# Rearranging the last part of a fused state-space and feed-forward kernel: an early quarter of a convolution, dense weights in four buffers, four dense products beside the last output product

## The chip, the cores and the metric

The kernel runs on one core of a Trainium2 chip as one launch. The metric is the device time in microseconds (us). Before the change it is 1575.42 us, the median of three runs (1573.84 to 1576.71).

## What is computed

The reference has two residual layers. The first mixes tokens with a gated state-space block, the second is a dense layer behind a grouped convolution, with a mask:

```python
# x: (64 sequences, 32 positions, 512 channels), float32
def reference(x, cond, ...):
    # layer 1: per-sequence 32x32 mixing, in-projection to 10304 channels, causal
    # convolution of 4 taps, SiLU, scan over 32 positions, gate, norm, out-projection
    x = x + attn(cond_mix(x, cond))
    # layer 2
    c2 = conv1d(x, weight9, groups=4) + cond @ c_weight.T + bias   # along the channels
    dots = softmax(c2 @ centroids.T / 0.1)                         # 64 centroids
    hits = dots > 0.01
    query_sel = any(hits, over centroids)        # one flag per token
    cluster_sel = any(hits, over all tokens)     # one flag per centroid
    row_sel = cluster_sel[assignments]           # one flag per output channel
    dense = c2 @ weight.T + ffn_bias
    return x + where(query_sel & row_sel, dense, 0)
```

`row_sel` needs the hits of all 2048 tokens, so no output can be written before the last token has been routed.

## The kernel before

**Layer 1.** The tokens are worked in 4 groups of 512 (T = 0 to 3), the 4096 inner channels in 8 groups (g = 0 to 7). That is 32 steps, i = 8 T + g. A step runs ten chunks (`chunk(i, c)`): each is a product of 12 matmuls (three passes over four 128-row pieces, because every float32 operand is split into a high and a low part), followed by an activation and, for eight of ten kinds, by tap or gate work on DVE and ACT. Between the chunks the step places the work of the step before it: `yend` (DVE multiplies the scan's result y by the gate, ACT makes the high part `yhi`, DVE subtracts to get `ylo`), `sumsq`, and the out-projection `out_step(i, 0..3)`, whose result `outp_end` adds to the accumulator `acc`. `inner(c)` places smaller things after chunk c: `gram`, the scan (L492), `decay`. `y_part` makes y in two halves.

**Order.** For PE and SP (the queue that issues nearly all DMAs) the order of the instructions is the order in which the program is written. On DVE, ACT and POOL a scheduler decides it when the program is built. Every engine and the SP queue execute in order: an instruction that waits holds all behind it on its engine.

**Buffers.** SBUF tiles with one tag share a fixed number of buffers; a new tile waits until the tile that held the buffer has been read for the last time. For what follows these matter: `raw` (4 buffers), `wsp` (7, the weights of the chunks), `y2` (3), `y` (3), `B` and `C` (2 each), `x` (4), `z` (6). PSUM has seven banks under the tag `mm` and one under `gs`.

**Layer 2, the tail.** It begins after step 31. 16 tiles of 128 tokens are numbered j = 0 to 15; a quarter is four tiles.
- `outp_end` of the steps with g = 7 stores `acc` to DRAM twice: as it is (`x1_d`, by POOL's queue) and turned (`x1p_d`, L669; in the last group 16 stores by SP).
- `p_load(j)` (L686) loads a turned tile, `conv(js)` (L758) runs the convolution of two or four tiles on PE and DVE adds the context (`c2s`, L768). `c2_xpose(j)` (L784) turns the tile back on PE; ACT makes the high part (L792) and DVE the low part (L793).
- `route(T)` multiplies a quarter with the centroids, `route2(T)` makes softmax, hits and `qsel` (the flag of each token).
- `asg_i` (L1011) loads the assignments; DVE makes from them `asg_f`, `oh` and `oh2`, a one-hot table (both in tag `B`).
- `dense(j)` is the dense product of tile j, 12 matmuls of about 2.7 us in all. `dense_kept` copies the result from PSUM to SBUF.
- After the last quarter's `route2`, 16 small matmuls count the hits (`cnt_ps`), another spreads the selected clusters (`r_ps`, L1076), ACT copies this to `rsel` and DVE makes `bm` = bias x rsel.
- `finish(j)`: DVE runs three instructions of 128x512: x1 += bm x qsel (L1085), d = dense x qsel x rsel (L1089), d += x1 (L1090); SP stores d.

In the kernel before, all 16 tiles' convolution lies behind the last chunk of step 31. The list `units` holds the order of the convolution, transposes and routing, and two dense products (tiles 0 and 1) are kept. The other 14 come after the last convolution:

```python
    j = NI - 1
    unit(1); y_part(j, 8, 16); unit(1)          # conv(0, 1), second half of y, conv(2, 3)
    ...yend, sumsq...
    unit(5); unit(2)                            # conv(4..7), four transposes, conv(8..11), route(0)
    for bg in range(4): out_step(j, bg)
    for k in range(4): unit(2); ...load and split dense weights wf[:, k]...
```
(line breaks are changed here.)

Of the kernel before, what the change touches and what calls it, by code (L numbers as in the profile page):

```python
# [7 lines left out]
F32 = mybir.dt.float32  # L8
# [24 lines left out]
def mamba_block_kernel(  # L33
# [641 lines left out]
    attend(0)  # L675
    w_ahead(-1)

    p_of, c2_of, ffn = {}, {}, {"next": 0}
    hits = {}

    def p_load(j):
        pr = sb.tile([P, 4, 130], F32, tag="wsp", name=f"pr{j}", bufs=7)
        T, jj = divmod(j, 4)
        nc.vector.memset(pr[:, :, 0:1], 0.0)
        nc.vector.memset(pr[:, :, 129:130], 0.0)
        nc.sync.dma_start(out=pr[:, :, 1:129], in_=x1p_d[T][jj])  # L686
        p_of[j] = pr
# [31 lines left out]
        for r in range(4):  # L719
            nc.vector.tensor_copy(cr[:, r], o[:, r])  # L720

    def split_load(src, shape, name, tg, bufs):
        raw = sb.tile(shape, F32, tag="raw", name=name + "r", bufs=4)
        nc.sync.dma_start(out=raw, in_=src)
        hi = sb.tile(shape, F32R, tag=tg, name=name + "h", bufs=bufs)
        lo = sb.tile(shape, F32R, tag=tg, name=name + "l", bufs=bufs)
        nc.scalar.copy(hi, raw)
        nc.gpsimd.tensor_tensor(lo, raw, hi.bitcast(F32), ALU.subtract)
        ffn[name] = (hi, lo)

    def ffn_start():
        ffn["qsel"] = const.tile([P, 16], F32, tag="qsel", name="qsel")

    def c2_tiles(T):
        if T < 2:
# [3 lines left out]
        return tuple(  # L739
            sb.tile([P, 4, TOK], F32R, tag=tg, name=f"c2_{T}_{tg}", bufs=nb) for tg, nb in tags  # L740
        )

    def p_more(n):
        for _ in range(n):
            j = ffn["next"]
            if j < 12:
                p_load(j)
                ffn["next"] = j + 1

    def conv(js):  # L750
        src = [p_of.pop(j) for j in js]
        o = [bank(f"cv{j}") for j in js]
        for d in range(3):
            for j, s, t in zip(js, src, o):
                for q in range(4):
                    at = 32 * ((q + j) % 4)
                    rows = slice(32 * q, 32 * q + 32)
                    nc.tensor.matmul(  # L758
                        t[at : at + 32].rearrange("p (b m) -> p b m", b=4),
                        lhsT=tww[rows, d, :],  # L760
                        rhs=s[rows, :, d : d + 128],
                        start=d == 0,
                        stop=d == 2,
                    )
        for j, t in zip(js, o):
            tg, nb = (("B", 2), ("C", 2), ("x", 4))[2 if j // 4 % 2 else j % 2]
            c2 = sb.tile([P, 4, P], F32, tag=tg, name=f"c2s{j}", bufs=nb)
            nc.vector.tensor_tensor(  # L768
                c2,
                t.rearrange("p (b m) -> p b m", b=4),  # L770
                ctxr[:, j].unsqueeze(2).to_broadcast([P, 4, P]),
                ALU.add,
            )
            ffn[("c2", j)] = c2
        p_more(len(js))

    def c2_xpose(j):
        T, jj = divmod(j, 4)
# [32 lines left out]
    def route2(T):  # L811
# [20 lines left out]
        nc.vector.tensor_scalar(hit, d, THRESHOLD, None, ALU.is_gt)  # L832
        nc.vector.tensor_reduce(ffn["qsel"][:, 4 * T : 4 * T + 4], hit, AX.X, ALU.max)
        hits[T] = hit

    def at(f, *a):
        return lambda: f(*a)

    units = [at(conv, (0, 1)), at(conv, (2, 3)), at(conv, (4, 5, 6, 7))]
    units += [at(c2_xpose, j) for j in range(4)]  # L840
    units += [at(conv, (8, 9, 10, 11)), at(route, 0)]
    units += [at(c2_xpose, j) for j in range(4, 8)]
    units += [at(route2, 0), at(route, 1)]
    units += [at(c2_xpose, j) for j in range(8, 12)]
    units += [at(route2, 1), at(route, 2)]
    units += [lambda j=j: dense_kept(j) for j in range(2)]
    units += [at(conv, (12, 13, 14, 15)), at(route2, 2)]
    units += [at(c2_xpose, j) for j in range(12, 16)]

    def unit(n=1):  # L850
        for _ in range(n):
            units.pop(0)()

    NI = NT * NG

# [27 lines left out]
    for i in range(NI):  # L883
# [9 lines left out]
        def inner(c):  # L893
            nonlocal wo_steps
            if c in (1, 2, 3, 4):
                if c < 4:
                    wo_split()
                next(wo_steps, None)
            if c in (5, 6):
                wo_store()  # L900
            if c == 6 and i + 1 < NI and (i + 1) % NG:
                da_load(i + 1)
            if c == 8:
                wo_steps = wo_pieces(i)
                for _ in range(1 if i + 1 < NI else 4):
                    next(wo_steps)
            if c == 3 + late:
                gram(i)
            if c == 4:
                flip(i, 0)  # L910
                if i:
                    scan(i)
            if c == 7:
                gram_rows(i)
                decay(i)
            if i == NI - 1 and c > 4:
                p_more(1)

        chunk(i, 0)
        if i and g == 0:  # L920
# [54 lines left out]
        step_more()  # L975
        if i == NI - 3:
            turned_setup()
            ffn_start()
        chunk(i, 9)
        inner(9)  # L980
        flip(i, 3)
# [1 line left out]
        step_more()  # L983
        y_part(i, 0, 8)

    j = NI - 1
    unit(1)
    y_part(j, 8, 16)
    unit(1)
    for c in range(4):  # L990
        yend(j, c)
    sumsq(j)
    split_load(cent, [P, 4, 64], "ct", "z", 6)
    unit(5)
    unit(2)
    for bg in range(4):
        out_step(j, bg)

    wf_t = sb.tile([P, 2, 4, DM], F32R, tag="wo", name="wf_t", bufs=1)
    wf_hi, wf_lo = wf_t[:, 0], wf_t[:, 1]  # L1000
    for k in range(4):
        unit(2)
        wr = sb.tile([P, DM], F32, tag="raw", name=f"wfr{k}", bufs=4)
        nc.sync.dma_start(out=wr, in_=wf[:, k, :])
        nc.scalar.copy(wf_hi[:, k, :], wr)
        nc.gpsimd.tensor_tensor(wf_lo[:, k, :], wr, wf_hi[:, k, :].bitcast(F32), ALU.subtract)

    for j in range(12, 16):
        p_load(j)
    asg_i = sb.tile([64, DM], mybir.dt.int32, tag="y2", name="asg_i", bufs=3)  # L1010
    nc.sync.dma_start(out=asg_i, in_=asg.partition_broadcast(64))  # L1011
    cl = const.tile([64, 2], F32, tag="cl", name="cl")
    nc.sync.dma_start(out=cl, in_=cl_in)
    asg_f = sb.tile([64, DM], F32, tag="y2", name="asg_f", bufs=3)
    nc.vector.tensor_copy(asg_f, asg_i)
    br = sb.tile([P, 2, DM], F32, tag="da", name="br", bufs=1)
    bias_b, rsel = br[:, 0], br[:, 1]
    nc.sync.dma_start(out=bias_b, in_=bf.partition_broadcast(P))
    oh = sb.tile([64, DM], BF16, tag="B", name="oh", bufs=2)
    nc.vector.tensor_scalar(oh, asg_f, cl[:, 0:1], None, ALU.is_equal)  # L1020
    oh2 = sb.tile([64, DM], BF16, tag="B", name="oh2", bufs=2)
    nc.vector.tensor_scalar(oh2, asg_f, cl[:, 1:2], None, ALU.is_equal)
    nc.vector.tensor_tensor(oh, oh, oh2, ALU.max)

    fo, x1t = {}, {}

    def x1_load(j):
        T, jj = divmod(j, 4)
# [7 lines left out]
    def dense(j, lo=0, hi=DM):  # L1036
        T, jj = divmod(j, 4)
        cols = slice(128 * jj, 128 * jj + 128)
        c2_hi, c2_lo = c2_of[T]
        o = bank(f"fo{j}_{lo}")[:, : hi - lo]  # L1040
        mm_split(
            o,
            lambda k: c2_hi[:, k, cols],
            lambda k: c2_lo[:, k, cols],
            lambda k: wf_hi[:, k, lo:hi],
            lambda k: wf_lo[:, k, lo:hi],
            4,
        )
        fo[(j, lo)] = o

    def dense_kept(j):
        dense(j)
        kept = sb.tile([P, DM], F32, tag="z", name=f"kept{j}", bufs=6)
        nc.scalar.copy(kept, fo[(j, 0)])
        fo[(j, 0)] = kept

    unit(len(units))
    for j in range(6):
        x1_load(j)
    route(3)  # L1060
    dense(2)
    route2(3)
    dense(3)
    late_ones, crep = ffn["late"][:, 1024:1152], ffn["late"][:64, 1152:1280]
    cnt_ps = ps.tile([64, 2], F32, tag="gs", name="cnt_ps", bufs=1)
    for n in range(16):
# [4 lines left out]
    csel = const.tile([64, 1], F32, tag="csel", name="csel")  # L1071
    nc.vector.tensor_scalar(csel, cnt_ps[:, 0:1], 0.5, None, ALU.is_gt)
    nc.vector.tensor_scalar(crep, late_ones[:64, :], csel, None, ALU.mult)
    dense(4)
    r_ps = ps.tile([P, DM], F32, tag="gs", name="r_ps", bufs=1)
    nc.tensor.matmul(r_ps, lhsT=crep, rhs=oh, start=True, stop=True)  # L1076
    nc.scalar.copy(rsel, r_ps)
    bm = sb.tile([P, DM], F32, tag="dt", name="bm", bufs=1)
    nc.vector.tensor_tensor(bm, bias_b, rsel, ALU.mult)

    def finish(j, lo=0, hi=DM):
        q = ffn["qsel"][:, j : j + 1]
        o = fo.pop((j, lo))
        x1 = x1t[j]
        nc.vector.scalar_tensor_tensor(  # L1085
            x1[:, lo:hi], bm[:, lo:hi], q, x1[:, lo:hi], ALU.mult, ALU.add
        )
        d = sb.tile([P, hi - lo], F32, tag="y", name=f"fd{j}_{lo}", bufs=3)
        nc.vector.scalar_tensor_tensor(d, o, q, rsel[:, lo:hi], ALU.mult, ALU.mult)  # L1089
        nc.vector.tensor_tensor(d, d, x1[:, lo:hi], ALU.add)  # L1090
        nc.sync.dma_start(
            out=out[4 * j : 4 * j + 4].rearrange("b s d -> (b s) d")[:, lo:hi], in_=d
        )

    for j in range(4, 16):
        if j + 2 < 16:
            x1_load(j + 2)
        finish(j - 4)
        if 4 < j < 15:
            dense(j)  # L1100
    dense(15, 0, 256)
    for j in range(12, 15):
        finish(j)
    dense(15, 256, 512)
    finish(15, 0, 256)
    finish(15, 256, 512)
# [96 lines left out]
```

## Time and profile before

| what | value |
|---|---|
| median of three runs | 1575.42 us |
| time of the profiled execution | 1577.95 us |
| its span, first to last instruction | 1576.2 us |
| granted TensorE clock, mean | 0.987 |
| PE busy, share of the span | 96% |
| DVE / ACT / POOL busy | 75% / 40% / 30% |
| last matmul of step 31's chunks ends | 1462.9 us |
| last matmul of the kernel ends | 1571.1 us |
| last DVE instruction ends | 1573.4 us |

A profile line of the timeline gives the start, the busy time, the engine, the source line, what is written and read, the number of instructions and, in brackets, the idle time ahead of them and what ended it. In a table by windows, each engine has its busy time in the window and the number of instructions. A row of the chain of waits has a start, a length and the engine whose work, or wait, the chain passes through. "issue" is waiting for which the profile shows no other cause.

### The profile page before, as it was taken

How to read it: one execution, taken by the hardware profiler on the slowest of the kernel's cores; microseconds unless marked ns; L12 is line 12 of the kernel's file. 1: busy time of each engine (PE TensorE's matmuls, PEld its weight loads, DVE VectorE, ACT ScalarE, POOL GpSimd, SP SyncE). 2: the span in 40 equal slices, each digit the busy share in tenths (PEclk: the TensorE clock that was granted, in tenths of full speed). 3: DMA queues.
4: the chain of work that ended last, by engine and by line, in shares of the span. 5: the costliest groups of instructions: out<-in, count | busy, mean ns of one | idle time of the engine just before them, and what ended most of it. 6: DMA issues, size and time to landing. Idle time of an engine off the chain costs nothing.

```text
span 1576.2 us, 35828 instructions
## 1 busy us (share of the span) xinstructions
PE 1519.7 (96%) x14963; PEld 1246.4 (79%) x14963; DVE 1180.3 (75%) x1877; ACT 629.4 (40%) x1122; POOL 476.7 (30%) x446
## 2 busy tenths in 40 slices
PE   6789999999999999999999999999999999999898
PEld 5567888788778888888888888888888888888567
DVE  5677777788866777977877777877877777777658
ACT  4455564455433333434433333434433333333230
POOL 6266665554341112222141112223141112222110
PEclk9789999999999999999999999999999999999999
DMA  5566888677575555555575555655575555554454
GB/s 190 175 237 212 308 309 292 194 233 279 185 241 184 176 171 179 198 191 171 191 241 190 165 180 169 209 176 175 187 245 188 170 181 167 182 179 139 119 164 167
DMA packets 124033, 311.71 MB, mean 198 GB/s; under 512 B 30880, under 2 KB 42400, under 8 KB 121824
## 3 DMA queue, kind: packets, MB, share of 16 engines
q1 hardware_dynamic: 121056, 302.08, 57.0%
q0 software_dynamic: 2816, 7.34, 1.4%
q8 instruction: 118, 1.93, 0.5%
q14 instruction: 43, 0.35, 0.1%
HBM read 237.54 MB, written 71.83 MB: 196 GB/s over the span
## 4 chain that ended last, share of the span: by engine, by line
PE 69%; DVE 17%; issue 4%; ACT 4%; POOL 3%; DMA 2%; SPq 1%; POOLq 0%; ACTq 0%; DVEq 0%
PE mm L192 42%; PE o L192 17%; PE y L549 5%; DVE x L447 3%; DVE ylo L577 2%; DVE src L492 1%; PE g_ps L503 1%; DVE acc L659 1%; DMA w<-in_win_dram 1%; DVE C L447 1%; DVE src L533 1%; POOL wsp L401 1%; DVE xs L463 1%; PE fo L192 1%; PE gr_ps L515 1%
## 5 line engine op out<-in xcount | busy, mean ns | idle before, releaser
L192 PE MATMUL mm<-hid,wsp 128*128 128x512 f32 x3840 | 931.6, 396 | 0.0
L192 PEld LDWEIGHTS mm<-hid,wsp 128*128 128x128 f32 x3840 | 721.1, 190 | 151.3 <-issue 1.0
L573 POOL TENSOR_TENSOR y<-y,y 128x512 f32<-128x512 f32 x96 | 145.3, 1514 | 547.9 <-ACT y L563 543.2
L447 DVE SCALAR_TENSOR_TENSOR x<-mm,xw,x 128x496 f32<-128x496 f32 (+2 forms) x384 | 272.2, 709 | 26.0 <-ACT x L443 20.9
L192 PE MATMUL o<-wo,yhi 128*128 128x512 f32 x1024 | 279.2, 394 | 8.8 <-POOL wo L631 6.2
L455 ACT ACTIVATE x<-x 128x512 f32<-128x512 f32 x128 | 81.0, 632 | 378.4 <-DVE x L447 355.1
L192 PEld LDWEIGHTS o<-wo,yhi 128*128 128x128 f32 x1024 | 190.2, 188 | 49.1 <-POOL wo L631 7.9
L447 DVE SCALAR_TENSOR_TENSOR B<-mm,pack,B 128x496 f32<-128x496 f32 (+2 forms) x96 | 68.7, 716 | 175.5 <-ACT B L443 173.3
L577 DVE TENSOR_TENSOR ylo<-z,yhi 128x512 fp32r<-128x512 f32 x128 | 141.4, 1108 | 1.0 <-ACT yhi L576 1.0
L443 ACT ACTIVATE x<-mm,xb,xw 128x512 f32<-128x512 f32 x128 | 99.7, 779 | 94.5 <-PE mm L192 93.5
L192 PE MATMUL o<-wo,ylo 128*128 128x512 f32 x512 | 137.1, 390 | 0.0
L549 PEld LDWEIGHTS y<-src,xs 32*64 32x64 f32 x8192 | 91.1, 132 | 41.9 <-issue 25.6
L463 DVE STREAM_TRANSPOSE xs<-x 128x512 f32<-128x512 f32 x128 | 89.8, 701 | 45.9 <-ACT x L455 43.5
L659 DVE SCALAR_TENSOR_TENSOR acc<-o,r,acc 128x512 f32<-128x512 f32 x128 | 95.3, 745 | 34.8 <-POOL r L601 30.3
L549 PE MATMUL y<-src,xs 32*64 32x32 f32 x8192 | 99.6, 227 | 18.1 <-DVE src L533 6.7
L601 POOL TENSOR_TENSOR r<-var,mhalf 128x4 f32<-128x4 f32 x32 | 33.2, 1039 | 269.4 <-DVE var L597 269.4
L192 PEld LDWEIGHTS o<-wo,ylo 128*128 128x128 f32 x512 | 96.1, 188 | 20.4 <-DVE ylo L577 0.2
L565 DVE SCALAR_TENSOR_TENSOR z<-y,pack,z 128x512 f32<-128x512 f32 x128 | 94.5, 742 | 19.3 <-ACT y L563 19.3
L401 POOL TENSOR_TENSOR wsp<-w,wsp 128x512 fp32r<-128x512 f32 x56 | 77.7, 1400 | 98.8 <-ACT wsp L400 69.7
L576 ACT CAST yhi<-z 128x512 fp32r<-128x512 f32 x128 | 78.9, 619 | 52.3 <-DVE z L565 52.2
L436 ACT ACTIVATE z<-mm 128x512 f32<-128x512 f32 x128 | 75.9, 593 | 56.4 <-PE mm L192 56.4
L447 DVE SCALAR_TENSOR_TENSOR C<-mm,pack,C 128x496 f32<-128x496 f32 (+2 forms) x96 | 68.8, 716 | 16.5 <-ACT C L443 14.3
(195 smaller groups left out, 1350.5 us busy)
## 6 DMA issues: line engine op xcount, KB each, us to landing
wsp<-wsp SPq DMA_DIRECT2D x320, 512.0 KB
wo<-wos SPq DMA_DIRECT2D x96, 512.0 KB
da<-da SPq DMA_DIRECT2D x128, 128.0 KB
wos<-wo SPq DMA_DIRECT2D x16, 1024.0 KB
w<-in_win_dram SPq DMA_DIRECT2D x48, 256.0 KB
wor<-in_wout_dram SPq DMA_DIRECT2D x32, 256.0 KB
xr<-in_win_dram SPq DMA_DIRECT2D x24, 256.0 KB
acc<-in_x_in_dram SPq DMA_DIRECT2D x4, 1024.0 KB
```

What stands on the lines that cost most here:

```text
L192: nc.tensor.matmul(o, lhsT=a(k), rhs=b(k), start=j == 0, stop=j == last)
L401: nc.gpsimd.tensor_tensor(lo, w, hi.bitcast(F32), ALU.subtract)
L443: nc.scalar.activation(t, o, AF.Identity, bias=bias, scale=taps[:, 3:4])
L447: nc.vector.scalar_tensor_tensor(tv[:, :, d:], ov[:, :, : L - d], taps[:, 3 - d : 4 - d], tv[:, :, d:], ALU.mult, ALU.add,)
L455: nc.scalar.activation(t, t, AF.Silu)
L463: nc.vector.transpose(st["xs"][:, :, k], t.rearrange("p (n t) -> p n t", t=L))
L549: nc.tensor.matmul(st["y"][q][64 * f : 64 * f + 64, 32 * n : 32 * n + 32], lhsT=st["xs"][r, n, 2 * f : 2 * f + 2].rearrange("p e x -> p (e ...
L565: nc.vector.scalar_tensor_tensor(z, y, nw_s[:, cc : cc + 1], z, ALU.mult, ALU.mult)
L573: st["add"] = nc.gpsimd.tensor_tensor(y2, st["y2"], y2, ALU.add).ins
L576: nc.scalar.copy(hi, z)
L577: st["lo"] = nc.vector.tensor_tensor(lo, z, hi.bitcast(F32), ALU.subtract).ins
L659: nc.vector.scalar_tensor_tensor(acc[:, bg, :], o, st["r"][:, bg : bg + 1], acc[:, bg, :], ALU.mult, ALU.add)
```

## The change

It rearranges the last two steps and the tail:

1. The convolution of tiles 0 to 3 and its transposes move into steps 30 and 31, between chunks. The centroids are loaded and split in step 30.
2. The dense weights have no buffer of their own in `wo` now. They are loaded in two DMAs of two pieces into one buffer `wr` and split into four `wsp` buffers (`wf_of[0..3]`): the first pair in step 31 after chunk 5, the second after chunk 8.
3. `p_load` uses the four `raw` buffers for all tiles but 8, 9 and 10.
4. `route(0)` moves between the two halves of the last y. Behind the second half come four dense products (tiles 0 to 3), then the out-projection, then `conv(4..7)`, the loads of tiles 12 to 15, the loads of assignments and the one-hot table, `conv(8..11)`, and the rest in the order shown.
5. Kept dense results (tiles 0 to 5) get the bias added on the way from PSUM, by DVE instead of ACT's copy. For the tiles from 6 on, `prep` adds bm x qsel to x1, with ACT and POOL. `finish` has two DVE instructions for each tile instead of three.

```diff
     def p_load(j):
-        pr = sb.tile([P, 4, 130], F32, tag="wsp", name=f"pr{j}", bufs=7)
+        tg, nb = ("wsp", 7) if j in (8, 9, 10) else ("raw", 4)
+        pr = sb.tile([P, 4, 130], F32, tag=tg, name=f"pr{j}", bufs=nb)
...
+    def ct_load():
...
+        nc.scalar.copy(ct[:, 0], raw)
+        nc.gpsimd.tensor_tensor(ct[:, 1], raw, ct[:, 0].bitcast(F32), ALU.subtract)
...
+    def wf_load(k):
+        if k == 0:
+            ffn["wr"] = sb.tile([P, 2, DM], F32, tag="wsp", name="wfr", bufs=7)
+        raw = ffn["wr"]
+        nc.sync.dma_start(out=raw, in_=wf[:, k : k + 2, :])
+        for n in range(2):
+            t = sb.tile([P, 2, DM], F32R, tag="wsp", name=f"wf{k + n}", bufs=7)
+            nc.scalar.copy(t[:, 0], raw[:, n])
+            nc.gpsimd.tensor_tensor(t[:, 1], raw[:, n], t[:, 0].bitcast(F32), ALU.subtract)
+            wf_of[k + n] = t
+
+    def bias_load():
+        br = sb.tile([P, 2, DM], F32, tag="da", name="br", bufs=1)
+        nc.sync.dma_start(out=br[:, 0], in_=bf.partition_broadcast(P))
...
     def conv(js):
...
-            tg, nb = (("B", 2), ("C", 2), ("x", 4))[2 if j // 4 % 2 else j % 2]
+            tg, nb = (("y", 3), ("x", 4), (("B", 2), ("C", 2))[j % 2], ("x", 4))[j // 4]
             c2 = sb.tile([P, 4, P], F32, tag=tg, name=f"c2s{j}", bufs=nb)
...
         def inner(c):
...
-            if i == NI - 1 and c > 4:
-                p_more(1)
+            if i == NI - 2:
+                if c == 4:
+                    for p in range(2):
+                        p_load(p)
+                    ct_load()
+                if c == 6:
+                    conv((0, 1))
+                    for p in range(2, 4):
+                        p_load(p)
+                if c in (7, 8):
+                    c2_xpose(c - 7)
+            if i == NI - 1:
+                if c == 3:
+                    conv((2, 3))
+                if c in (4, 5):
+                    c2_xpose(c - 2)
+                if c > 4 and c < 9:
+                    if c % 3 == 2:
+                        wf_load(2 * (c // 8))
+                    p_load(c - 1)
+                if c == 9:
+                    bias_load()
...
     def dense_kept(j):
         dense(j)
-        kept = sb.tile([P, DM], F32, tag="z", name=f"kept{j}", bufs=6)
-        nc.scalar.copy(kept, fo[(j, 0)])
+        e = sb.tile([P, DM], F32, tag="z", name=f"kept{j}", bufs=6)
+        nc.vector.tensor_tensor(e, fo[(j, 0)], ffn["br"][:, 0], ALU.add)
...
+    j = NI - 1
+    route(0)
+    y_part(j, 8, 16)
+    for c in range(4):
+        yend(j, c)
+    sumsq(j)
+    for p in range(8, 12):
+        p_load(p)
+    for b in range(4):
+        dense_kept(b)
+    for bg in range(4):
+        out_step(j, bg)
+    conv((4, 5, 6, 7))
+    for p in range(12, 16):
+        p_load(p)
+    asg_i = sb.tile([64, DM], mybir.dt.int32, tag="y2", name="asg_i", bufs=3)
+    nc.sync.dma_start(out=asg_i, in_=asg.partition_broadcast(64))
...
+    oh = sb.tile([64, DM], BF16, tag="B", name="oh", bufs=2)
+    nc.vector.tensor_scalar(oh, asg_f, cl[:, 0:1], None, ALU.is_equal)
+    oh2 = sb.tile([64, DM], BF16, tag="B", name="oh2", bufs=2)
+    nc.vector.tensor_scalar(oh2, asg_f, cl[:, 1:2], None, ALU.is_equal)
+    nc.vector.tensor_tensor(oh, oh, oh2, ALU.max)
+
+    conv((8, 9, 10, 11))
+    for b in range(4, 8):
+        c2_xpose(b)
+    route2(0)
+    for b in range(8, 12):
+        c2_xpose(b)
+    route(1)
+    route(2)
+    route2(1)
+    conv((12, 13, 14, 15))
+    route2(2)
+    dense_kept(4)
+    for b in range(12, 16):
+        c2_xpose(b)
     for j in range(6):
         x1_load(j)
+    dense_kept(5)
     route(3)
-    dense(2)
+    dense(6)
     route2(3)
-    dense(3)
+    dense(7)
...
-    dense(4)
+    dense(8)
...
+    def prep(j):
+        t = sb.tile([P, DM], F32, tag="y2", name=f"bq{j}", bufs=3)
+        nc.scalar.activation(t, bm, AF.Identity, scale=ffn["qsel"][:, j : j + 1])
+        nc.gpsimd.tensor_tensor(x1t[j], x1t[j], t, ALU.add)
+
     def finish(j, lo=0, hi=DM):
...
-        nc.vector.scalar_tensor_tensor(
-            x1[:, lo:hi], bm[:, lo:hi], q, x1[:, lo:hi], ALU.mult, ALU.add
-        )
...
+    def finish_to(n):
+        nonlocal done
+        while done < n:
+            if done + 6 < 16:
+                x1_load(done + 6)
+                prep(done + 6)
+            finish(done)
+            done += 1
+
+    for j in range(9, 15):
+        finish_to(2 * (j - 8))
+        dense(j)
     dense(15, 0, 256)
-    for j in range(12, 15):
-        finish(j)
+    finish_to(15)
     dense(15, 256, 512)
     finish(15, 0, 256)
     finish(15, 256, 512)
```

More of the change, by code (lines that the diff above doesn't have):

```diff
@@ L676, in mamba_block_kernel @@
     w_ahead(-1)
-    p_of, c2_of, ffn = {}, {}, {"next": 0}
+    p_of, c2_of, ffn = {}, {}, {}
     hits = {}
     def p_load(j):
-        pr = sb.tile([P, 4, 130], F32, tag="wsp", name=f"pr{j}", bufs=7)
+        tg, nb = ("wsp", 7) if j in (8, 9, 10) else ("raw", 4)
+        pr = sb.tile([P, 4, 130], F32, tag=tg, name=f"pr{j}", bufs=nb)
         T, jj = divmod(j, 4)
@@ L720, in turned_setup @@
             nc.vector.tensor_copy(cr[:, r], o[:, r])
[L722 to L731, printed above, removed]
-        ffn["qsel"] = const.tile([P, 16], F32, tag="qsel", name="qsel")
+    def ct_load():
+        raw = sb.tile([P, 4, 64], F32, tag="raw", name="ctr", bufs=4)
+        nc.sync.dma_start(out=raw, in_=cent)
+        ct = sb.tile([P, 2, 4, 64], F32R, tag="dt", name="ct", bufs=1)
+        nc.scalar.copy(ct[:, 0], raw)
+        nc.gpsimd.tensor_tensor(ct[:, 1], raw, ct[:, 0].bitcast(F32), ALU.subtract)
+        ffn["ct"] = (ct[:, 0], ct[:, 1])
+        ffn["qsel"] = const.tile([P, 16], F32, tag="qsel", name="qsel")
+    wf_of = {}
+    def wf_load(k):
[11 more added lines that the diff above has]
+        nc.sync.dma_start(out=br[:, 0], in_=bf.partition_broadcast(P))
+        ffn["br"] = br
     def c2_tiles(T):
@@ L741, in c2_tiles @@
         )
[L743 to L748, printed above, removed]
     def conv(js):
@@ L774, in conv @@
             ffn[("c2", j)] = c2
-        p_more(len(js))
     def c2_xpose(j):
@@ L834, in route2 @@
         hits[T] = hit
[L836 to L852, printed above, removed]
     NI = NT * NG
@@ L977, in mamba_block_kernel @@
             turned_setup()
-            ffn_start()
         chunk(i, 9)
@@ L984, in mamba_block_kernel @@
         y_part(i, 0, 8)
[L986 to L1025, printed above, removed]
+    fo, x1t, kept = {}, {}, set()
     def x1_load(j):
@@ L1044, in dense @@
             lambda k: c2_lo[:, k, cols],
-            lambda k: wf_hi[:, k, lo:hi],
-            lambda k: wf_lo[:, k, lo:hi],
+            lambda k: wf_of[k][:, 0, lo:hi],
+            lambda k: wf_of[k][:, 1, lo:hi],
             4,
@@ L1052, in dense_kept @@
         dense(j)
-        kept = sb.tile([P, DM], F32, tag="z", name=f"kept{j}", bufs=6)
-        nc.scalar.copy(kept, fo[(j, 0)])
-        fo[(j, 0)] = kept
-    unit(len(units))
+        e = sb.tile([P, DM], F32, tag="z", name=f"kept{j}", bufs=6)
+        nc.vector.tensor_tensor(e, fo[(j, 0)], ffn["br"][:, 0], ALU.add)
+        fo[(j, 0)] = e
+        kept.add(j)
+    j = NI - 1
[15 more added lines that the diff above has]
+    nc.sync.dma_start(out=asg_i, in_=asg.partition_broadcast(64))
+    cl = const.tile([64, 2], F32, tag="cl", name="cl")
+    nc.sync.dma_start(out=cl, in_=cl_in)
+    asg_f = sb.tile([64, DM], F32, tag="y2", name="asg_f", bufs=3)
+    nc.vector.tensor_copy(asg_f, asg_i)
+    bias_b, rsel = ffn["br"][:, 0], ffn["br"][:, 1]
+    oh = sb.tile([64, DM], BF16, tag="B", name="oh", bufs=2)
[17 more added lines that the diff above has]
+        c2_xpose(b)
     for j in range(6):
         x1_load(j)
+    dense_kept(5)
     route(3)
-    dense(2)
+    dense(6)
     route2(3)
-    dense(3)
+    dense(7)
     late_ones, crep = ffn["late"][:, 1024:1152], ffn["late"][:64, 1152:1280]
@@ L1083, in finish @@
         o = fo.pop((j, lo))
-        x1 = x1t[j]
-        nc.vector.scalar_tensor_tensor(
-            x1[:, lo:hi], bm[:, lo:hi], q, x1[:, lo:hi], ALU.mult, ALU.add
-        )
         d = sb.tile([P, hi - lo], F32, tag="y", name=f"fd{j}_{lo}", bufs=3)
         nc.vector.scalar_tensor_tensor(d, o, q, rsel[:, lo:hi], ALU.mult, ALU.mult)
-        nc.vector.tensor_tensor(d, d, x1[:, lo:hi], ALU.add)
+        nc.vector.tensor_tensor(d, d, x1t[j][:, lo:hi], ALU.add)
         nc.sync.dma_start(
@@ L1093, in finish @@
         )
[L1095 to L1100, printed above, removed]
+    done = 0
+    def finish_to(n):
[9 more added lines that the diff above has]
+        dense(j)
     dense(15, 0, 256)
-    for j in range(12, 15):
-        finish(j)
+    finish_to(15)
     dense(15, 256, 512)
```

## The prediction

> **What bounds the kernel now.** I began with the page's busy shares: PE is busy for 96% of the span. Up to 1462.9 us the chain of waits is one unbroken row of PE products, so whatever is put on PE there, or makes PE wait there, moves the end by as much. Then I took the engines by windows over the end:
>
> ```profile
> 1460.00:1480.00 20.00, 16.91 (x472) 10.13 (x471) 11.56 (x23) 6.35 (x13) 5.88 (x4) 1.00 0.76 225
> 1480.00:1500.00 20.00, 18.28 (x159) 12.07 (x157) 11.68 (x36) 2.23 (x5) 2.21 (x3) 1.00 0.14 44
> 1500.00:1520.00 20.00, 18.19 (x105) 12.94 (x112) 13.70 (x27) 10.13 (x18) 6.26 (x6) 1.00 0.76 208
> 1520.00:1540.00 20.00, 18.29 (x183) 12.54 (x183) 9.95 (x24) 4.14 (x8) 0.00 (x0) 1.00 0.26 79
> ```
>
> The columns are PE, weight loads, DVE, ACT, POOL, granted clock, DMA share, GB/s. The clock is 1.00 throughout. PE loses time in every window. The PE timeline names the gaps: 2.15, 0.94, 1.72, 0.45, 0.47, 0.90 and 1.54, in sum 8.17 us. That is all the rearrangement can win on PE, since it leaves the matmuls as they are. The last matmul ends at 1571.1, DVE at 1573.4, and the last store takes 2.8 us more (span 1576.2).
>
> Next I read what decides whether a new order fits: the SP queue and DVE, both in order. First the SP timeline, then DVE's in two places:
>
> ```profile
> 1496.16 10.59 SPq L669 DMA_DIRECT2D x1p<-acc  x16
> ...
> 1508.92 2.60 SPq L686 DMA_DIRECT2D pr<-x1p  x4
> 1511.58 1.82 SPq L1011 DMA_DIRECT2D asg_i<-in_asg_dram  x1
> ```
>
> ```profile
> 1427.86 2.22 DVE L447 SCALAR_TENSOR_TENSOR C<-mm,pack,C 128x496 f32<-128x496 f32 x3 [0.49 <-ACT C L443]
> ...
> 1442.88 2.28 DVE L492 TENSOR_TENSOR_SCAN src<-da,src 128x1024 f32<-128x1024 f32 x1
> ...
> 1518.16 0.42 DVE L1015 CAST asg_f<-asg_i 64x512 f32<-64x512 int32 x1 [0.88 <-DMA asg_i<-in_asg_dram]
> ```
>
> The 16 stores of the turned last group keep SP for 10.6 us, and asg_i cannot be issued before them. In step 31 DVE runs from 1427.9 to the scan's end at 1445.1 with one gap, 0.59 us: it is behind PE there.
>
> **The change, part by part.** Times below are in the profiled execution (span 1576.2; its own time is 1577.95, 2.5 above the median of 1575.42). I work out the shift of the span and add it to the median. The order of instructions comes from the built programs.
>
> *Moved convolution.* conv(0,1), conv(2,3) and four transposes go from the tail into steps 30 and 31: 2 x 2.73 + 4 x 0.46 = 7.3 us of PE later there, 7.3 less in the tail: zero. Of the gaps, all 8.17 us belong to places that are rebuilt, so I take them as gone: **-8.2**. The 2.15 ("issue", inside the second half of y) has no cause in the profile and may come back: 0 to 2.2. conv(8..11) took 5.0 us among other waits, conv(12..15) 3.2: I take **-1.0** (0 to -1.8).
>
> *A new wait in step 31.* PE's order becomes gram, conv(2,3), chunk 4, transpose of tile 2. DVE's built order puts c2s of tile 2 behind the scan. Before, the gram's last matmul was followed by chunk 4 at 1434.98. The added PE work of step 30 (2.73 + 0.9 = 3.6) shifts this to 1438.6; conv 2.73 and chunk 4's 2.72 bring PE to the transpose at 1444.05. DVE is shifted by 3.6 as well: scan's end 1445.1 + 3.6 - 0.66 (a tap now behind it) = 1448.0, c2s 0.62 more: 1448.65. **+4.6**. Queued behind this transpose on PE is chunk 5 and with it the whole kernel. I bound it by one DVE instruction: 4.0 to 5.2. The same wait in step 30 is covered: c2s of tile 0 is done near 1409, PE comes at 1411.8.
>
> *Second pair of dense weights.* Its DMA stands on SP behind the four loads of wo (2 MB), which wait for step 30's last out-projection. Before, those were issued from 1460.2; by the windows of 2 us, 2.6 MB had moved 8.9 us after that. The same from 1472.0 gives 1480.9. y ends at 1480.5 (1462.8 + 7.3 + 4.6 = 1474.7, and 1.45 + 2.83 + 1.45). ACT and POOL still split it (0.62 and 1.33 each), so the first dense product ends about 1484.7 instead of 1483.2: **+1.5**, 0 to 5.7 (if the loads move at 200 GB/s rather than 300 or more). ACT's squares of y stand behind these splits, but the four dense products (4 x 2.74) cover them, with about 1 us over; before, DVE needed 10.5 us from y's end to the end of `part`.
>
> *pr11 waits for conv(4..7).* Tile 11 now takes the `raw` buffer of tile 4, so it waits for cv4, which PE runs only behind the last out-projection. cv11 is due 1.7 us after cv4, and the load needs 0.6 issue and 2.2 landing: **+1.1** (0 to 2). It also stands ahead of the 16 stores on SP. Before, they were issued while PE did the out-projection, from the first `acc` on.
>
> *asg_i, the largest term.* From the end of cv4, SP issues pr11 (0.6), 16 stores (10.6), four loads (2.6), asg_i (1.8), and that lands 2.2 later: 17.8 us. The 2.2 is the 2.8 from issue to landing of the x<-acc stores less their 0.6 of issue; before, asg_i itself took up to 6.6 from issue, behind other loads, which bounds the sum to 16.6 to 20.3. On DVE, asg_f, oh, oh2 and max (1.8), a sum and a reciprocal (0.65) and c2s of tile 8 (0.66) follow: 20.9 us. c2s of tile 8 must wait for oh2, because both take a `B` buffer; and behind asg_f in DVE's order stands all else that quarter 2 needs. PE's transpose of tile 8 waits for it. PE arrives 8.4 us after cv4 (rest of both convolutions 6.1, four transposes 1.84, lt 0.45). **+12.5** (11.3 to 15). Tile 10's c2s takes tile 8's buffer only after its transpose: **+0.8** (0 to 1.3). Both routings, conv(12..15) and ten dense products are queued behind it.
>
> *PE's end:* 1571.1 - 8.2 - 1.0 + 4.6 + 1.5 + 1.1 + 12.5 + 0.8 = 1582.4.
>
> *The finish.* Four more dense products are done early, so behind r_ps PE has seven left, 7 x 2.74 = 19.2 us (before eleven, 30.4). DVE has two instructions for each tile: rsel and bm 1.3, then 16 x (0.66 + 0.60) = 20.2, together 21.5 after r_ps. This is 2.3 behind PE, as before. But x1 is now made by ten POOL additions of two SBUF tiles beside it. The nearest row, ylo, has two SBUF inputs as `d + x1` has, and runs beside POOL's additions of the same size:
>
> ```profile
> L577 DVE TENSOR_TENSOR ylo<-z,yhi x28: 669/1125/1766, 1216.1 to 1479.4; 128x512 fp32r<-128x512 f32 x28
> ```
>
> Least 0.67, median 1.13: 0.46 more for ten tiles is **+4.6**, and DVE ends 6.9 behind PE. Below, nothing: 2.3. Above, POOL and DVE strictly in turn: ten additions of 1.4, and of DVE 16 x 0.60 and six kept tiles' products of 0.66, 27.6 and the 1.3: 9.7. Three `y` buffers add no more than this: a tile's store must land (2.8) before its buffer is used again, so three tiles take 4.1 us, 1.4 each. The bias on kept tiles costs DVE 6 x 0.66 where it waits for PE anyway.
>
> [...]
>
> *Sum:* 1582.4 + 6.9 + 2.8 = 1592.1, that is 15.9 above 1576.2; on the median **1591 us**, 1.0% slower. All low ends: 1571.1 - 8.2 - 1.8 + 15.3 + 2.3 + 2.8 = 1581.5, or 1581 on the median. All high ends reach 1606.
>
> **Rivals.**
> - *A, not slower: asg_i does not hold quarter 2.* If the one-hot table is ready when PE reaches tile 8's transpose, 13.3 falls away: 1578 us, within 0.2% of before. It decides from the point at which asg_i lands: it would have to land 5.2 us after cv4. For it speaks only that POOL, ACT and DVE have room there. Against it, the SP rows: after 5.2 us SP has issued seven of the 16 stores. Chance 0.06.
> - *B, all waits are covered and the gaps are filled.* PE ends at 1571.1 - 8.2 - 1.0 + 1.5 = 1563.4, DVE 2.3 later, store 2.8: 1568.5, on the median 1568. For it: four dense products, 11 us, stand where 4.8 us were lost, and DVE loses 16 x 0.66 in the finish. Against it: both DVE orders. Chance 0.05.
> - *C, slower still: DVE and POOL in turn, or the weights late.* 2.8 and up to 4.2 more, and the "issue" gap again: 1594 to 1601, middle 1597. Chance 0.19.
> - The forecast, with its neighbours between 1579 and 1594: 0.70.
>
> **How the numbers follow.** 1591 is the likeliest case. The range goes from 1581 (all low ends) to 1601 (C); A and B and the last part of C, some 0.15, are left out. 0.2% is 3.2 us, about what a measurement here can tell from no change. Faster: B and a little of A, 0.06. Same: the rest of A, 0.05. Slower: 0.89.
>
> **What would show it.** In the profile after: a PE idle of about 4 to 5 us ahead of a transpose (L792) in step 31, put down to DVE; one of 11 to 15 us ahead of a transpose in the tail, with DVE's asg_f (L1048) idle for a DMA at that time; the 16 stores of L669 starting only after conv(4..7); `d + x1` (L1104) with a mean near 1 us; the last matmul some 7 us ahead of the last DVE instruction. It is wrong if DVE reaches c2s of tile 8 before PE needs it, or if DVE ends within 3 us of PE.

## The result, and the profile after

The changed kernel takes **1601.34 us** (median of four runs, 1599.75 to 1606.12), the kernel before, beside it, 1574.66 (1573.84 to 1576.71). The ratio is 1.0173, with a 95% interval of 1.0148 to 1.0197: slower, as forecast, but by 26.7 us instead of 16, and 1601.34 lies just beyond the end of the range.

The profiled execution has a span of 1598.8 us (1576.2 before). Both kernels do the same work up to `turn_ps` (the context's turning, on PE); executions differ by some us before it, so I measure from its start. From there to the end the kernel before takes 203.1 us and the changed one 229.4: **+26.3**. The waits of PE behind that point, each with its sum, number and longest:

```profile
PE ctp L792 <- DVE c2s L777: 14.9, 2, 10.4
PE fo L192 <- DVE fd L1103: 4.5, 1, 4.5
PE cv L767 <- DMA pr<-x1p: 2.7, 1, 2.7
PE y L549 <- issue: 1.7, 1, 1.7
```

The timeline of PE says where they lie. In brackets is the wait ahead of the row:

```profile
1445.32 1.12 PE L792 MATMUL ctp<-back,c2s 128*128 128x128 f32 x4 [4.46 <-DVE c2s L777]
...
1480.11 0.68 PE L549 MATMUL y<-src,xs 32*64 32x32 f32 x43 [1.68 <-issue]
...
1512.19 4.70 PE L767 MATMUL cv<-pr,tww 32*32 32x512 f32 x72 [2.69 <-DMA pr<-x1p]
...
1529.58 3.84 PE L792 MATMUL ctp<-back,c2s 128*128 128x128 f32 x16 [10.41 <-DVE c2s L777]
...
1579.12 2.07 PE L192 MATMUL fo<-wf,c_yhi 128*128 128x512 f32 x4 [4.54 <-DVE fd L1103]
```

In sum 23.8 us of waiting, where the kernel before had 8.3. Look also at the second number, the busy time: 16 transposes take 3.84 us (1.91 and 1.97 elsewhere in this trace), four matmuls of a dense product 2.07 (1.07 elsewhere). The windows behind three of these waits say why. The columns are PE, weight loads, DVE, ACT, POOL, granted clock, DMA share, GB/s:

```profile
1445.30:1449.50 4.20, 4.18 (x15) 3.53 (x16) 3.27 (x9) 1.10 (x2) 1.29 (x1) 0.66 0.00 0
1449.50:1455.00 5.50, 5.50 (x28) 4.55 (x27) 1.31 (x2) 2.11 (x4) 1.28 (x1) 1.00 0.01 1
...
1529.50:1537.00 7.50, 7.42 (x32) 5.57 (x33) 4.36 (x8) 2.92 (x5) 0.00 (x0) 0.73 0.01 2
1537.00:1545.00 8.00, 8.00 (x121) 4.86 (x120) 4.90 (x12) 1.00 (x2) 0.00 (x0) 1.00 0.11 35
...
1579.00:1584.00 5.00, 4.88 (x12) 3.81 (x13) 4.69 (x7) 1.44 (x2) 2.28 (x3) 0.50 0.84 263
```

Behind a wait the granted clock falls, to 0.50 in the last window, and is back at 1.00 some 3 to 6 us after the wait's end. In the trace's clock records the low stretches are 3.41, 3.41, 3.41, 10.24 and 6.83 us long, each at 0.50. Summed over windows of 1 us from `turn_ps` to the last matmul (busy time times the missing share of the clock), PE loses **9.55 us** in this way: 1.41, 1.71, 1.71, 1.95 and 2.78 behind the five waits. The kernel before loses 0.00 there.

DVE's rows show what the 4.46 us in step 31 were: the first transpose (at 1445.32) waits for `c2s`, which stands behind the scan, as forecast.

```profile
1442.27 2.28 DVE L492 TENSOR_TENSOR_SCAN src<-da,src 128x1024 f32<-128x1024 f32 x1
1444.58 1.29 DVE L777 TENSOR_TENSOR c2s<-cv,ctxr 128x512 f32<-128x512 f32 x2
```

The SP queue and DVE show the chain that I had forecast for the 10.4 us:

```profile
1474.29 34.44 SPq L687 DMA_DIRECT2D pr<-x1p  x4
1508.83 10.87 SPq L669 DMA_DIRECT2D x1p<-acc  x16
1519.80 2.64 SPq L687 DMA_DIRECT2D pr<-x1p  x4
1522.49 0.67 SPq L1044 DMA_DIRECT2D asg_i<-in_asg_dram  x1
```

```profile
1526.72 0.42 DVE L1048 CAST asg_f<-asg_i 64x512 f32<-64x512 int32 x1 [5.32 <-DMA asg_i<-in_asg_dram]
```

pr11 stands on SP until cv4 is done; the stores, four loads and asg_i follow one by one, and DVE waits.

In the finish, POOL's additions and DVE's instructions for tiles 4 and 5 stand against each other like this:

```profile
1571.53 6.33 POOL L1097 TENSOR_TENSOR x1s<-x1s,bq 128x512 f32<-128x512 f32 x4 [4.34 <-DMA x1s<-x]
```

```profile
1572.01 1.37 DVE L1103 SCALAR_TENSOR_TENSOR fd<-kept,qsel,br 128x512 f32<-128x512 f32 x1 [0.65 <-DMA out_dram<-fd]
1573.41 1.66 DVE L1104 TENSOR_TENSOR fd<-fd,x1s 128x512 f32<-128x512 f32 x1
1574.99 1.75 DVE L1103 SCALAR_TENSOR_TENSOR fd<-kept,qsel,br 128x512 f32<-128x512 f32 x1
1576.77 1.64 DVE L1104 TENSOR_TENSOR fd<-fd,x1s 128x512 f32<-128x512 f32 x1
1578.33 0.74 DVE L1103 SCALAR_TENSOR_TENSOR fd<-fo,qsel,br 128x512 f32<-128x512 f32 x1
```

Four additions one after the other take 6.33 us, 1.58 each, and beside them each DVE instruction takes 1.4 to 1.75 instead of 0.69 to 0.75. The last row, which reads the dense result from PSUM, takes 0.74, though an addition (1578.52 to 1579.79) runs beside it. It is also tile 6's first, and frees the bank for which dense product 13 waits at 1579.12. The groups of the finish show the same as means (busy us, mean ns):

```profile
L1104 DVE TENSOR_TENSOR fd<-fd,x1s 128x512 f32<-128x512 f32 (+1 forms) x17 | 16.7, 989 | 1.2
L1103 DVE SCALAR_TENSOR_TENSOR fd<-fo,qsel,br 128x512 f32<-128x512 f32 (+1 forms) x11 | 7.6, 693 | 0.0
L1103 DVE SCALAR_TENSOR_TENSOR fd<-kept,qsel,br 128x512 f32<-128x512 f32 x6 | 6.0, 1015 | 0.8 <-DMA out_dram<-fd 0.7
```

Held up are those with two large SBUF inputs, `d + x1` (up to 1.78 us) and the products of the kept tiles (up to 1.75); the products that read the dense result from PSUM are not (0.75 at most).

Who waits for whom in the finish? These are DVE's waits from r_ps to its end:

```profile
DVE bm L1092 <- ACT br L1090: 3.5, 1, 3.5
DVE fd L1103 <- DMA out_dram<-fd: 0.7, 1, 0.7
```

The first is the wait for `rsel`, which the kernel before has too (3.5 us, the greater part of it ahead of r_ps). None is for PE. So the finish hangs on DVE alone: the 4.54 us that PE waits there, and the 2.78 us of clock behind them, did not move the end. From r_ps to DVE's last instruction the changed kernel takes 32.9 us, the kernel before 33.0: the finish, which was to become shorter, is as long as it was. Nearly all of the +26.3 arose ahead of r_ps, where four dense products more (11.0 us) now stand.

### The profile page after: what moved, and what is told of

Same layout as the page of the kernel before. It is cut to its first block, busy times and chain, and to the rows that moved or that the text cites. A ratio compares the mean times of both kernels' runs of the same rounds, so it can differ in the third digit from the quotient of the medians.

```text
span 1598.8 us, 35863 instructions
## 1 busy us (share of the span) xinstructions
PE 1524.2 (95%) x14963; PEld 1251.2 (78%) x14963; DVE 1181.0 (74%) x1866; ACT 634.9 (40%) x1130; POOL 489.2 (31%) x456
## 4 chain that ended last, share of the span: by engine, by line
PE 68%; DVE 13%; issue 6%; DMA 5%; POOL 4%; ACT 2%; SPq 1%; POOLq 0%; DVEq 0%; ACTq 0%
PE mm L192 41%; PE o L192 16%; PE y L549 5%; DVE x L447 3%; POOL wsp L401 2%; DMA w<-in_win_dram 2%; PE fo L192 2%; DVE ylo L577 1%; DVE src L492 1%; PE g_ps L503 1%; PE cv L767 1%; DVE acc L659 1%; DMA wor<-in_wout_dram 1%; PE lo L192 1%; PE gr_ps L515 1%
## 5 line engine op out<-in xcount | busy, mean ns | idle before, releaser
L565 DVE SCALAR_TENSOR_TENSOR z<-y,pack,z 128x512 f32<-128x512 f32 x128 | 94.6, 742 | 22.1 <-ACT y L563 19.3
```

Source lines behind the costliest of these rows:

```text
L565: nc.vector.scalar_tensor_tensor(z, y, nw_s[:, cc : cc + 1], z, ALU.mult, ALU.mult)
```

## The experiments

My theory after this result had three parts: PE's waits are those of in-order queues (c2s behind the scan; asg_i behind pr11, cv4 and the stores); each costs its length and a stretch of low clock; POOL's additions hold up DVE, and through a bank PE. The rivals: the four dense products and the late weights are the cost; the slow finish alone; slow transposes have another cause. "From turn_ps" is the distance from the start of turn_ps to the end of the span.

**The one-hot table early.** The block from asg_i to the `max` is written ahead of the loads of tiles 8 to 11:

```diff
+    asg_i = sb.tile([64, DM], mybir.dt.int32, tag="y2", name="asg_i", bufs=3)
+    ...   # cl, asg_f, oh, oh2, max
     for p in range(8, 12):
         p_load(p)
```

> The changed kernel with asg_i, cl and the one-hot table (L1043 to L1054) moved ahead of the loads of pr8 to pr11; nothing else. Theory (the ctp wait of tile 8 comes from asg_i behind the 16 stores, and each PE wait of over 3 us also costs what PE loses at a lower granted clock right behind it): the wait of 10.4 us in the tail is gone, and the 16 transposes behind it take 1.9 instead of 3.8 us, so 12 to 13 us less than the changed kernel: 1588 to 1590 us. Rival 1 (c2s of tile 8 is held by something else as well, cv11 or tile 4's transposes): under 5 us less, 1596 or more. Rival 2 (only the wait counts and the clock's part is given back in the finish, where DVE, not PE, sets the end): 8 to 10.5 us less, 1591 to 1593.

Measured: 1590.02 us (1587.46 to 1596.0), ratio 1.0096 (1.0068 to 1.0124) to the kernel before; from turn_ps 213.9, 15.5 less than the changed kernel. The wait is gone:

```profile
1519.76 1.09 PE L792 MATMUL ctp<-back,c2s 128*128 128x128 f32 x8
1521.33 1.09 PE L792 MATMUL ctp<-back,c2s 128*128 128x128 f32 x8 [0.47 <-DVE c2s L777]
```

The chain to asg_i is the cause of the largest wait. The clock loss falls to 3.41 us; two of the low stretches besides this one are missing here, since waits of 1.89 and 2.01 us did not bring the clock down in this execution. Their 3.4 us are part of the 15.5, so the time does not part the theory from rival 2; the transposes do: eight take 1.09 us, and the clock is 1.00.

**PE's work moved into the wait.** `route(1)`, `dense_kept(4)` and `dense_kept(5)` go between the transposes of tiles 7 and 8, SP is left as it is.

```diff
     route2(0)
+    route(1)
+    dense_kept(4)
+    dense_kept(5)
     for b in range(8, 12):
         c2_xpose(b)
```

> The changed kernel with PE's work moved instead of the load: routing of tile group 1 and the dense products 4 and 5 stand between the transposes of tiles 7 and 8. Theory: 8.4 us of work (2.9 + 2 x 2.74) lie in the 10.4 us wait, about 2 us of wait stay, PE keeps its clock, and some 2 us come back where the dense products covered c2s of tile 12 and the low parts of tile 15: 7 to 9 us less than the changed kernel, 1592 to 1594. Rival (the wait moves, since DVE's order puts c2s of tile 8 later, or the places that are laid open wait as long): under 4 us less, 1597 or more.

Measured: 1598.7 us (1595.1 to 1600.95), ratio 1.0144 (1.0121 to 1.0167); from turn_ps 224.3, 5.1 less, which lies between theory and rival. In the time (2.6 us less) the rival was right: beside 2.79 us ahead of tile 8, waits of 1.72, 0.67 and 1.54 us came up where the moved work had covered c2s and the low parts. Cover that is taken elsewhere is paid for there.

**The transposes of tiles 2 and 3 two chunks later.**

```diff
-                if c in (4, 5):
-                    c2_xpose(c - 2)
+                if c in (6, 7):
+                    c2_xpose(c - 4)
```

> The changed kernel with the transposes of tiles 2 and 3 in step 31 two chunks later (at chunks 6 and 7 in place of 4 and 5). Theory: the wait of 4.5 us behind the scan is gone and the 0.66 clock behind it too, 5 to 6 us less than the changed kernel: 1595 to 1596. Rival (DVE is the engine that is behind in step 31, so PE waits for it later in the step): the wait comes up again at another line, less than 2 us gained, 1599 or more.

Measured: 1593.41 us (1590.68 to 1599.94), ratio 1.0125 (1.0091 to 1.0158); from turn_ps 221.7, 7.7 less. The wait of 4.46 is gone and none came up in its place in step 31, so the rival falls. The 7.7 is not the wait and its clock alone (4.46 + 1.41): the wait for cv11 was shorter too (1.78), the clock did not fall behind it, and the finish took 1.6 less. Against that, the wait for c2s of tile 8 grew to 13.35, since PE came to it earlier.

**Dummy work in the wait.** Three, and in a second kernel four, further dense products of tile 0 that nobody reads stand ahead of tile 8's transposes.

```diff
     route2(0)
+    for n in range(3):   # 4 in the second
+        warm(n)          # dense product of tile 0 into a bank of its own
     for b in range(8, 12):
```

> The changed kernel with three further dense products of tile 0, which nobody reads, between the transposes of tiles 7 and 8, that is 8.2 us of PE work inside the 10.4 us wait; the wait for c2s of tile 8 itself stays as it is. Theory (the idle PE gets a lower clock): about 2 us of wait remain, the 16 transposes behind it take about 1.9 instead of 3.84 us at a granted clock near 1.0 (0.73 before), and the time is 1 to 3 us less than the changed kernel, though PE does more. Rival (transposes are slow because they wait for DVE's c2s and for one another's buffers): they take 3.5 to 4 us as before, and the time is the same.

With three: 1602.98 us, from turn_ps 229.4, no gain. 2.71 us of wait remained, and the clock still fell behind it, to 0.50 from 1534 to 1537; only the low stretch now met the routing's matmuls instead of the transposes. That leaves both theories standing. With four no wait is left:

> The changed kernel with four dummy dense products (11 us) in the 10.4 us wait ahead of tile 8's transposes, so that PE has no pause there at all. Theory (the clock falls for a time after a pause of PE): from the first transpose of tile 8 to conv(12) 8.5 us, as in the run with the early one-hot table, in place of 9.8, at a granted clock of 1.0, and no wait but tile 10's. Rival (that stretch is paced by DVE and ScalarE): 9.8 us or more.

```profile
1526.52 1.03 PE L792 MATMUL ctp<-back,c2s 128*128 128x128 f32 x8
1527.90 1.09 PE L792 MATMUL ctp<-back,c2s 128*128 128x128 f32 x8 [0.35 <-DVE c2s L777]
...
1534.83 3.46 PE L767 MATMUL cv<-pr,tww 32*32 32x512 f32 x96
```

From the first transpose to conv(12) 8.31 us, against 9.76 in the changed kernel, with the clock at 1.00: the slow transposes are the clock's, and 1.45 us of that stretch. (1595.08 us, one run; from turn_ps 228.9.) In the changed kernel's trace the falls take 1.41 to 1.95 us behind four of its waits and 2.78 behind the last; waits of 1.68 and 2.69 us were followed by one as well as those of 4.46 us and more. What sets a fall off, and what ends it, is not shown.

**The finish without POOL, and with DVE alone.** In the first kernel `prep` is left out, so that the bias's share is missing in the output of tiles 6 to 15. In the second DVE adds it, as in the kernel before:

```diff
     def finish(j, lo=0, hi=DM):
+        if j not in kept:    # second kernel only
+            x1 = x1t[j][:, lo:hi]
+            nc.vector.scalar_tensor_tensor(x1, bm[:, lo:hi], q, x1, ALU.mult, ALU.add)
...
-                prep(done + 6)
```

> The changed kernel without prep: no product on ScalarE and no addition on POOL in the finish, so the output lacks the bias's share (bm times q) in tiles 6 to 15. Taken from the end of turn_ps, so that the executions' offset falls out. Theory (the finish is slow because POOL's additions hold up both DVE instructions of every tile, and tile 6, thereby late, holds the bank that dense product 13 needs): from r_ps to DVE's end about 23 us in place of 33, no PE wait ahead of dense 13, and 9 to 10 us less than the changed kernel. Rival (the finish is paced by the y buffers and the stores' landing, or by the loads of x1 in SP's order): 29 us or more from r_ps, and under 4 us less.

> The changed kernel with the bias added on DVE for the ten tiles 6 to 15 (the scalar_tensor_tensor of the kernel before), nothing on POOL or ScalarE in the finish. Theory (POOL's ten additions cost DVE more than doing them itself): 1.3 + 6 x 1.29 + 10 x 1.95 = 28.5 us from r_ps to DVE's end in place of 33, the wait ahead of dense 13 under 1 us, about 4.5 us less than the changed kernel. [...]

From r_ps to DVE's end the changed kernel takes 32.9 us; without prep 26.8, with DVE alone 30.0 (times 1595.46 and 1599.05 us, one run each; from turn_ps 225.1 and 228.6, with r_ps some 2 us later because of longer low-clock stretches ahead of it). The 6.1 us that go without prep are some 5.5 for POOL's ten additions and 0.6 for `bm`, which the first kernel leaves out as well. The additions are dearer than ten more DVE instructions. The wait of dense 13 shrinks from 4.54 to 0.63 and 1.99. POOL's share is shown, but my 23 was too low, and from turn_ps the first kernel gains some 4 us where the theory had 9 to 10. The rival's `y` buffers have a part in it: three waits for a store to leave its buffer add 2.7. And without any POOL work a tile takes DVE 1.4 to 1.6 us and not 1.26: the addition starts 0.78 us after the product that it reads and the next product 0.61 later, where I had 0.66 and 0.60 from the kernel before, in which another instruction stands between the two:

```profile
1573.99 0.75 DVE L1095 SCALAR_TENSOR_TENSOR fd<-kept,qsel,br 128x512 f32<-128x512 f32 x1 [1.51 <-DMA out_dram<-fd]
1574.78 0.69 DVE L1096 TENSOR_TENSOR fd<-fd,x1s 128x512 f32<-128x512 f32 x1
```

**The mended kernel.** Early one-hot table, later transposes, no `prep`; the bias of tiles 4 to 15 goes into PSUM by one more product, whose two rows hold the high and low part of the bias.

```diff
+        if j > 3:
+            nc.tensor.matmul(o, lhsT=neg, rhs=bs[:, lo:hi], start=True, stop=False)
```

> The changed kernel with three edits together: the one-hot table early, the transposes of tiles 2 and 3 two chunks later, and prep taken out, with the bias of tiles 4 to 15 put into PSUM by one further PE product of two rows (0.23 us each). Theory: the single gains add up. From the end of turn_ps 229.4 - 15.5 - 7.7 (both measured) - 9.5 (finish without POOL) + 1.1 (five more PE products ahead of r_ps) = 197.8 against 203.1 before: 5 us less than before, 1569 to 1571 us. Rival (the waits only move on, so that the one is covered by the other): 1575 us or more.

Measured: 1578.67 us (1575.14 to 1583.84), ratio 1.0019 (1.0000 to 1.0038); from turn_ps 206.5 instead of 197.8, so the forecast of 1569 to 1571 was missed. Two things account for the 8.7. The two-row product cost 0.67 us a tile instead of 0.23 (3.41 us from one dense product to the next, against 2.74): 12 x 0.44 = 5.3 us. And waits of 1.77 (y) and 2.60 (cv11) brought 3.3 us of clock loss. Without these the single gains add up.

In the next kernel pr11 takes a `z` buffer:

```diff
-        tg, nb = ("wsp", 7) if j in (8, 9, 10) else ("raw", 4)
+        tg, nb = ("wsp", 7) if j in (8, 9, 10) else (("z", 6) if j == 11 else ("raw", 4))
```

> The three edits of the run before, and pr11 takes a z buffer in place of tile 4's raw buffer, so that it needn't wait for cv4 and the 16 stores need not wait for it. Theory: the wait of cv11 (1.8 to 2.7 us in all runs so far) is gone: 2 us less than with the three edits, 1567 to 1569. Rival (cv11's wait is due to the transfers, not to the buffer, or the wait comes up again at conv(12..15) or in the finish): no difference, under 0.7 us.

Measured: cv11's wait is gone; from turn_ps 201.3, 5.2 less, and 0.00 clock loss. But the time is 1576.41 us (1573.78 to 1582.58), ratio 1.0018 (1.0003 to 1.0032), only 2.3 less. In the next, tiles 6 to 8 are kept too, with their bias from DVE ahead of r_ps, the product has 128 rows, and d alternates between `y` and `y2`:

> The run before it (four edits) with three more in the finish: tiles 6 to 8 get their bias on DVE ahead of r_ps and are kept in C and B buffers as tiles 0 to 5 are, the bias product on PE is left for tiles 9 to 15 alone and has 128 rows (two of them filled) in place of 2, and the products d take turns in six buffers in place of three. Theory: the two-row product cost 0.67 us a tile in the trace in place of the 0.23 I had taken, so five of them less bring r_ps 3.4 us earlier; behind r_ps DVE is the bound with 1.6 + 16 x 1.40 = 24 us and no wait for stores, where it took 25.9: 5 us less than the run before it, 196 us from turn_ps against 203.1 in the kernel before: 1570 to 1572 us, 0.2 to 0.3% faster than the kernel before. Rival (DVE, the loads of x1 or the stores in SP's order set the finish): no gain over the run before it, 1575 or more.

From turn_ps 197.3, near the 196 of the theory: 5.8 less than the kernel before. The 128-row product costs 0.27 us a tile. But the time, 1573.98 us (1570.67 to 1579.11), ratio 0.9996 (0.9981 to 1.0010), is the same as before. So something was lost *ahead* of turn_ps, where the instructions are the same. The main loop has a part of it: its steady steps, some 15 of the 32, take 43.23 us in these two kernels and 42.98 to 43.00 in all the others so far. Two kernels tell whether pr11's buffer does this:

> The run before it but for the buffer of pr11: src in place of z. Measured from turn_ps the run before it was 5.8 us shorter than the kernel before, in the time only 1.5: in its trace a step of the main loop, whose code is the same, lasts 43.23 us in place of 42.99, in all other runs without pr11 in z 42.98 to 43.00. A z buffer then has 2080 bytes in place of 2048, so that all that lies behind z in SBUF moves by 192 bytes. Theory (the places in SBUF cost the 0.24 us a step): steps of 43.0 us, and about 27 x 0.24 = 6 us less than the run before it: 1567 to 1570 us, 0.35 to 0.5% faster than the kernel before. Rival (the steps' length is the execution's, or that of the tail's other edits): 43.2 us again, 1573 or more.

> The kernel before with a single edit: the two kept tiles are declared 520 wide and used to 512, so that a z buffer has 2080 bytes; every instruction and its order are those of the kernel before. Theory (places in SBUF): 43.2 us a step, 5 to 7 us slower than the kernel before, 1580 to 1583. Rival (the places make no difference): 43.0 us a step, and 1574 to 1577.

With pr11 in `src`: **1566.87 us** (1564.91 to 1568.92), ratio **0.9934** (0.9909 to 0.9959), faster than the kernel before (1574.82 beside it); 195.7 from turn_ps, steady steps of 43.00. The kernel before with wide `z` buffers: 1581.23 us (1579.14 to 1585.19), ratio 1.0034 (1.0017 to 1.0050), steady steps of 43.19 us. Both speak for the theory: with 32 bytes more in a buffer's size, which move all that lies behind `z`, the steady steps are 0.19 to 0.24 us longer. The size of it was forecast wrongly: not 27 steps change but some 15 (those of 44 us and more hardly change), which makes 3 to 4 us. The times differ by 6 to 7 us (1581.2 against 1574.8, and 1574.0 against 1566.9); in the traces 1.6 to 1.9 of this lie behind turn_ps, with a fall of the clock behind a wait in `y` (1.41 and 2.65 us), and the rest is not traced. One chunk between an out-projection and the next product, first in the kernel before, then with wide `z`:

```profile
1227.14 2.88 PE L192 MATMUL mm<-hid,wsp 128*128 128x512 f32 x12
```

```profile
1226.24 2.92 PE L192 MATMUL mm<-hid,wsp 128*128 128x512 f32 x12
```

Which of the moved tiles does it stays open. The best kernel keeps the four early dense products and the late weights, so the rival that these are the cost falls. The waits of PE from turn_ps on in the best kernel:

```profile
PE y L548 <- issue: 1.5, 1, 1.5
PE cnt_ps L1093 <- DVE late L839: 0.5, 1, 0.5
PE ctp L791 <- DVE c2s L776: 0.5, 1, 0.5
```

## Why the prediction was wrong in size

The sign, the places and the largest wait were right. **The step that failed is the sum "PE's end: 1571.1 - 8.2 - 1.0 + 4.6 + 1.5 + 1.1 + 12.5 + 0.8 = 1582.4"**: it lets every wait cost its own length. The clock behind the waits, for which the sum has no term, took 9.55 us, 6.77 of them ahead of r_ps, where they delay all that follows. **A second step failed as much, the finish**: 19.2 + 6.9 = 26.1 us from r_ps to DVE's end, where 32.9 were measured.

I read "the clock is 1.00 throughout" from the windows from 1460 on, and did not ask what longer waits would do to it; from turn_ps on the longest wait before was 2.15. But the same trace shows the price at an earlier place, within a `y`:

```profile
403.15 1.57 PE L549 MATMUL y<-src,xs 32*64 32x32 f32 x120 [2.61 <-DVE xs L463]
```

From 404.2 to 407.6 us the granted clock of the kernel before is 0.50 there.

Point by point:
- *Wait in step 31*, 4.6: measured 4.46, and 1.41 of clock. Moving the transposes showed it.
- *"issue" gap in y*, taken as gone: 1.68 came back, as the lower bound allowed. Its cause is still open; 1.4 to 2.7 us are there in every run.
- *Second pair of weights*, 1.5: the four products took 13.19 instead of 10.96 us, 1.71 of it clock. In the kernel without low clock (pr11 in `z`) they took 11.91, so the weights cost half a microsecond to one.
- *pr11*, 1.1 (0 to 2): 2.69, and 1.71 of clock. The wait for cv4 was right; but PE went on at 1512.19, 3.5 us after SP's row ends at 1508.73, where I had put down 2.2 for the landing.
- *asg_i*, 12.5 (11.3 to 15) and 0.8 for tile 10: 10.41 and 1.95 of clock, and no wait of its own for tile 10. SP's chain was right to about a microsecond (18.9 us from cv4's end to asg_f, forecast 17.8); PE came later than forecast, through cv11 and the clock.
- *The finish, "PE has seven left, 7 x 2.74 = 19.2 us"*: PE took 27.3 from r_ps. I had DVE wait for PE, never PE for DVE: tile 6 holds the bank of dense 13 until DVE has read it (4.54, and 2.78 of clock). But DVE never waits for PE in return, so this cost the end nothing. What counts is DVE's own row, forecast as 21.5 + 4.6. The 4.6 for POOL was nearly right (some 5.5). The 21.5 was not: without POOL's work, and with `bm`, DVE needs 26.8 + 0.6 = 27.4. I had each tile at 1.26 us, and the waits for stores, which I had put at nothing, were 2.7 in that run. The mean of `d + x1`, 0.99, is as forecast; but the kept tiles' products, 1.02 in the mean, I had left out. In the stretch shown both instructions of a tile were held, and each lasted about as long as one addition (1.37 to 1.75, against 1.58): there the forecast's upper bound, POOL and DVE strictly in turn, was nearer than the row of `ylo`.

Together: 26.3 passes the forecast's 15.9 by 10.4. Up to r_ps the sum had 22.8 us more than before (1582.4 - 19.2, against 1540.4), and 26.2 were measured: 3.4 of the 10.4. The waits there grew from 8.3 to 19.3, by 11.0, and the terms for them had 10.8 (4.6 + 1.1 + 12.5 + 0.8 - 8.2). That these agree so well is luck: single terms were off by up to 2 us, in both directions. The clock added 6.8, and all else came out some 3.5 below the sum. About 2 of these have a name: the late weights (0.5 instead of 1.5) and the convolutions (1.9 less than before instead of 1.0); the rest is open. The finish has 6.8 of the 10.4, and the last store 0.1.

Rival C ("DVE and POOL in turn, or the weights late, and the issue gap again", 1594 to 1601) came nearest in size, but by luck: the gap came back, POOL cost 0.9 more than forecast and the weights less, and the two main reasons, the clock and DVE's time for a tile without POOL, it does not have.

## What to carry to other kernels

Price a wait on PE as its length plus what the clock takes behind it, here 1.4 to 2.0 us for each of the four waits ahead of r_ps, and look in the windows' clock column of the whole trace for places below 1.00. Before that, ask which engine the end hangs on: in the finish it was DVE, and there 4.54 us of waiting on PE, with 2.78 of clock, cost nothing. When an order is rearranged, follow the in-order DMA queue to its last small load: 0.7 us of issue for an assignment table held the whole kernel for 10 us, and writing it ahead of four other loads gave 11 of the lost 27 us back. If a trace shows a gain that the time does not, compare a stretch whose instructions did not change.

## What was not expected of the hardware

- From turn_ps on, in all traces here, every wait of PE of 2.2 us or more was met or followed by a lower granted clock; of waits of 1.4 to 2.15 us some were (1.41, 1.46, 1.51, 1.65, 1.68, 1.77, 2.06) and some were not (1.50, 1.54, 1.69, 1.72, 1.78, 1.89, 1.91, 1.99, 2.01, 2.15).
- In the kernel with three edits a bias product of two rows, ahead of a dense product of 128, cost 0.67 us for 512 columns; filled up with rows of zeros to 128 it cost 0.27 in the kernel with nine kept tiles.
- 32 bytes more in the size of one tag's six buffers made each steady step of the main loop 0.2 us longer (43.19 us instead of 42.98), though no instruction changed.
